# Class tokens of layer 1's feed-forward: both grouped products before their sums over groups, and the output's sums after the first chunk of patches

## The chip, the cores and the metric

The kernel runs on one core of a Trainium2 chip. The core has five engines that work side by side, each through its own queue in order: TensorE (PE; its weight loads are shown apart as PEld), VectorE (DVE), ScalarE (ACT), GpSimd (POOL) and SyncE (SP), which here only issues DMAs. The metric is the device time of one execution in microseconds. The profile is one further execution, recorded by the hardware profiler; times in it count from the start of its span.

## What is computed

The whole program is a network of four layers on a state `x` of 512 nodes by 768 features; each layer has a graph part, an attention part and a feed-forward part. The change lies in the feed-forward part of the second layer, called layer 1. It treats the first six rows (class tokens) and the other 506 rows (patches) differently. Cut to that:

```python
cls_tokens   = x[:, :6]                  # of the normalised x
patch_tokens = x[:, 6:]
patch_out = gelu(patch_tokens @ fc1_w.T + fc1_b) @ fc2_w.T + fc2_b      # 768 -> 192 -> 768
gate_logits = einsum('bnd,nrd->bnr', l2norm(cls_tokens), l2norm(gate_pair)) + balance_bias
route_probs = softmax(gate_logits);  chosen_route = argmax(route_probs)
hid_all = gelu(einsum('bnd,ahd->bnah', cls_tokens, atom_in_w) + atom_in_b)   # five atoms of 192
# the chosen route takes one atom of hid_all, multiplies it by that route's atom_out_w,
# adds atom_out_b, and weighs it with the route's probability
cls_out = chosen_cand * chosen_w
return concatenate([cls_out, patch_out])     # is added to x
```

## The kernel before

**Tiling.** `x` lies token-major: four chunks `t` of 128 tokens, each in two halves `c` of 384 features. Its normalised form `xf` is turned by TensorE into `xfT`, feature-major, six blocks of 128 features (`Norm.first` and `Norm.rest`, two token chunks each; transposes at L274, evacuations at L205 and L207, the scaling itself at L254). All arithmetic is fp32; a matmul shows up as two passes in the trace.

**The class tokens' two products.** Six rows would use only six columns of TensorE. So `in_groups` (L372) deals the terms of a product over three groups of 32 columns: term `k` goes to group `k % 3`, and the three groups accumulate in three strips of one PSUM bank (L377). ScalarE copies the 96 rows to a tile `at_p` (L379). A second, small matmul with the matrix `three` then adds the three strips up (L1680 for the input product, L1771 for the output product), and VectorE adds the result to its place (L1681 to the atoms' `ha`, L1772 to `cls`, which holds the class tokens' rows of `x`). Each product is done in two halves: the input one by 480 of its 960 columns, with six terms each, the output one by 384 of 768 columns, with eleven terms each (ten of 96 rows, from `hT` and the weights `wo`, and one of five rows, the biases, from `cbT`).

**What lies between.** After the input product come the gate (squares L1695, scaling L1701, dot products L1704, softmax and choice to L1716), the coefficients (L1720 to L1723) and the mixing of the atoms (L1749, L1751), nearly all on VectorE with six rows; then ten small transposes (L1757) and a copy (L1758) that make `hT`. The patches' first product, fc1 (L298 and L1738, GELU at L1734 and L1742), gives `hid` beside that.

**The patches' second product.** `from_192` (L314) goes over the four chunks `t`: two matmuls (L320) and two on half of the rows (L323), then `use(t, c, ps)` for both halves: add to `x` (L332), for `t == 0` overwrite the six class rows with `cls` (L1785), and take the statistics of the next norm (L230), after whose second half the norm's small steps follow (L242 to L253) and the scaling on ScalarE (L254). Transposes of the first two chunks (L274) and the products of layer 2's graph part (L557) come next.

**Order, buffers and loads.** Each engine's order is fixed when the program is built, roughly in program order, with ready work drawn forward. PSUM has eight banks, asked for by `psum()`. `at_p` and the rows of biases (`row(...)`, L168) share a pool of two buffers. Weights rotate through three large buffers: the atoms' two input halves, fc1's weights, the atoms' two output halves (L148), fc2's (L1776, L1778), then layer 2's graph weights (L156) and, in one of them, `graph` (L1802). A load waits on SP until the last reader of its buffer is done, and what is behind it on SP waits too. Row `f1_b2` is added to `x` on POOL (L337), chunk by chunk after the chunk's `xf` is made.

Of the kernel before, what the change touches and what calls it, by code (L numbers as in the profile page):

```python
# [22 lines left out]
KC = D // P  # L23
HC = D // 2
# [73 lines left out]
def kernel(ctx: ExitStack, tc: tile.TileContext, a: dict, out: bass.AP):  # L98
    nc = tc.nc
    V, S, G, T = nc.vector, nc.scalar, nc.gpsimd, nc.tensor  # L100
# [20 lines left out]
    def w_tile(name="w", held=None):  # L121
        pool, n = turn_ = turns.pop(0)
        (turns if held is None else held).append(turn_)
        return pool.tile([P, KC * D], FP, tag="w" + n, name=name)

    def psum():
        return psp.tile([P, 512], FP, tag="ps", name="ps")
# [15 lines left out]
    def weights(src, p=P):  # L143

        k, n = src.shape[0] // p, src.shape[1]
        w = w_tile()
        v = w[:, : k * n].rearrange("p (k n) -> p k n", k=k)
        nc.sync.dma_start(v[:p], src.rearrange("(k p) n -> p k n", p=p))  # L148
        return v
# [9 lines left out]
    def spread(src, offset, n, parts=P):  # L159

        return bass.AP(tensor=src.tensor, offset=src.offset + offset, ap=[[0, parts], [1, n]])

    def row_tile(name, n=D):
        return rowp.tile([P, KC * (P + 2)], FP, tag="row", name=name)[:, :n]
# [128 lines left out]
    def feature_product(w, xT, f, width=P):  # L293

        ps = psum()
        n = xT.shape[1]
        for k in range(n):
            T.matmul(ps[:width], w[:, k, f : f + width], xT[:, k, :], start=k == 0, stop=k == n - 1)  # L298
        return ps[:width]

    def token_product(parts, w_of, use, then=None):

        n = len(parts)
        for t in range(NT):
            for c in range(2):
                ps = psum()[:, :HC]
                for k in range(n):
                    T.matmul(ps, parts[k][:, ts(t, P)], w_of(k)[:, ts(c, HC)],  # L308
                             start=k == 0, stop=k == n - 1)
                use(t, c, ps)  # L310
                if then:
                    then(t, c)

    def from_192(hid, wa, wb, use):  # L314


        for t in range(NT):
            bank = [psum()[:, :HC] for _ in range(2)]
            for c in range(2):
                T.matmul(bank[c], hid[:, 0, ts(t, P)], wa[:, ts(c, HC)], start=True, stop=False,  # L320
                         skip_group_check=True)
            for c in range(2):
                T.matmul(bank[c], hid[ts(c, HD), 1, ts(t, P)], wb[ts(c, HD), ts(c, HC)], start=False,  # L323
                         stop=True, skip_group_check=True)
            for c in range(2):
                use(t, c, bank[c])
# [4 lines left out]
    def add_to_x(t, c, ps):  # L331
        V.tensor_add(x[:, t, ts(c, HC)], x[:, t, ts(c, HC)], ps)  # L332
# [28 lines left out]
    G3 = 3 * 32  # L361
    three = const.tile([P, 8], FP, name="three")
# [9 lines left out]
    def in_groups(terms, n, name):  # L372


        ps = psum()[:G3, :n]
        for k, (l, r) in enumerate(terms):
            T.matmul(ps[ts(k % 3, 32)], l, r, start=k < 3, stop=k + 3 >= len(terms), skip_group_check=True)  # L377
        part = row_tile(name, n)
        S.copy(part[:G3], ps)  # L379
        return part[:G3]  # L380
# [804 lines left out]
    xfT, xs, rest = n.T, n.split, n.rest  # L1185
    with tc.tile_pool(name="ffn0", bufs=2) as fp:
# [120 lines left out]
        ps = feature_product(wi, xfT, 2 * P)  # L1307
# [115 lines left out]
    with tc.tile_pool(name="gat1", bufs=1) as gp:  # L1423
# [45 lines left out]
        def use(t, c, ps):  # L1469
            evacuate(h[:, t, 4 * c : 4 * c + 4, :HW], ps.rearrange("p (i c) -> p i c", i=4))  # L1470
# [174 lines left out]
        for t in range(NT):  # L1645
            z = tiny(1, name="ga_z1")
            for c in (1, 0):
                n = HC + c
                ps = psum()[:, :n]
                for s in range(NT):  # L1650
                    T.matmul(ps, ed[0].wT[t][:, s, :], h2[:, s, c * HC : c * HC + n],  # L1651
                             start=s == 0, stop=s == NT - 1)
# [11 lines left out]
    xf, xfT = nf.n, nf.T  # L1664
    with tc.tile_pool(name="ffn1", bufs=1) as fp:
        NCLS, NA, H = 6, 5, 192
        C = NCLS
# [5 lines left out]
        ha = fp.tile([C, NA, H], FP, name="ha")  # L1673
        hf = ha.rearrange("p a h -> p (a h)")
        nc.sync.dma_start(hf, spread(a["L1_ffn_atom_in_b"], 0, NA * H, C))
        for i in range(2):
            w = weights(a["L1_ffn_atom_in_w"][:, ts(i, 480)])
            part = in_groups([(xfT[:, k, :32], w[:, k, :]) for k in range(KC)], 480, "at_p")
            ps = psum()[:C, :480]
            T.matmul(ps, three[:G3, :C], part, start=True, stop=True)  # L1680
            V.tensor_add(hf[:, ts(i, 480)], hf[:, ts(i, 480)], ps)  # L1681
# [51 lines left out]
        ps = feature_product(w1, xfT, 0)  # L1733
        S.activation(hid[:, 0, :], ps, AF.Gelu, bias=col("f1_b1", 0))  # L1734
        ps = psum()[:, :HT]
        for k in range(KC):
            for i in range(2):
                T.matmul(ps[ts(i, HD)], w1[:, k, P : P + HD], xfT[:, k, ts(i, HT)],  # L1738
                         start=k == 0, stop=k == KC - 1, skip_group_check=True)
# [15 lines left out]
        ps = psum()[:HW, : 2 * NA * C].rearrange("p (k n) -> p k n", k=2 * NA)  # L1755
# [3 lines left out]
        cbT = fp.tile([NA, 32], FP, name="cbT")  # L1759
        G.memset(cbT, 0.0)  # L1760
        ps = psum()[:NA, :C]
        T.transpose(ps, cb, ident[:C, :C])
        V.tensor_copy(cbT[:, :C], ps)
        ab = big1[:NA, 0, :]
        nc.sync.dma_start(ab, a["L1_ffn_atom_out_b"])
        wo = [weights(a["L1_ffn_atom_out_w"][i * 480 : (i + 1) * 480, :], HW) for i in range(2)]
        for c in range(2):
            terms = [(hT[:, k, :], wo[k // NA][:HW, k % NA, ts(c, HC)]) for k in range(2 * NA)]
            part = in_groups(terms + [(cbT, ab[:, ts(c, HC)])], HC, "at_p")
            ps = psum()[:C, :HC]  # L1770
            T.matmul(ps, three[:G3, :C], part, start=True, stop=True)  # L1771
            V.tensor_add(cls[:, ts(c, HC)], cls[:, ts(c, HC)], ps)  # L1772


# [7 lines left out]
        def use(t, c, ps):  # L1782
            add_to_x(t, c, ps)
            if t == 0:
                V.tensor_copy(x[:C, 0, ts(c, HC)], cls[:, ts(c, HC)])  # L1785
            n2.part(t, c)

# [83 lines left out]
    xfT, xs, rest = nf.T, nf.split, nf.rest  # L1871
# [106 lines left out]
    xf, xfT = nf.n, nf.T  # L1978
# [7 lines left out]
    with tc.tile_pool(name="ffn3", bufs=1) as fp:  # L1986
# [48 lines left out]
        ps = psum()[:, : NT * E].rearrange("p (t e) -> p t e", t=NT)  # L2035
# [29 lines left out]
        ps = psum()[:, : NT - 1]  # L2065
        for j in range(NT - 1):
            for t in range(NT):
                T.matmul(ps[:, j : j + 1], to_slot[:, t, ts(j, P)], pid[:, t : t + 1],
                         start=t == 0, stop=t == NT - 1, skip_group_check=True)
# [6 lines left out]
        for ks in (range(4), range(4, KC)):  # L2076
            ps = psum()
            for i, k in enumerate(ks):
                for t in range(NT):
                    T.matmul(ps[:, ts(i, P)], xf[:, t, ts(k, P)], to_first[:, t, :],  # L2080
                             start=t == 0, stop=t == NT - 1, skip_group_check=True)
# [174 lines left out]
```

## Time and profile before

| | us |
|---|---|
| median of 3 runs | 3020.36 |
| lowest, highest | 3019.77, 3020.73 |
| the profiled execution | 3019.09 |
| its span | 3017.1 |
| PE busy in the span | 2937.0 |
| L377, the four grouped products: first start to last end | 1668.23 to 1701.63 |
| L320, first start | 1702.99 |
| L557, first product of layer 2's graph part | 1715.80 |

The profiled execution is 1.27 us below the median and 0.7 below the lowest of the timed runs. The stretch that the change touches is some 50 us out of the span. To read the views: the page's first part gives busy time by engine; the chain follows the work that ended last back from release to release, so an engine's share there is time in which the end waited for it; the timeline lists instructions in order of start, with an engine's idle time before one in brackets and what ended it; the windows give busy time by engine in a stretch, and the clock that TensorE was granted (1.00 is full).

### The profile page before, as it was taken

The page shows a single profiled execution, that of the slowest core. Times are in us where ns is not written, and L with a number is a line of the kernel's source. Part 1 is how long each engine was busy: PE and PEld are TensorE (multiplying, and loading weights), DVE is VectorE, ACT ScalarE, POOL GpSimd, SP SyncE. Part 2 cuts the span into 40 slices and gives each one's busy share as a digit, 9 for nine tenths or more (in the row PEclk, how much of TensorE's full clock was granted, in tenths as well). Part 3 has the DMA queues.
Part 4 walks back from the last instruction along what each step waited for, and adds up shares of the span by engine and source line. Part 5 has one row for each costly group of instructions (what it writes and reads, how often), then busy time and mean ns, then how long its engine had stood idle before and what let it go on. Part 6 is the DMA issues. An engine that isn't in the chain of part 4 may idle for free.

```text
span 3017.1 us, 31655 instructions
## 1 busy us (share of the span) xinstructions
PE 2937.0 (97%) x11721; PEld 1979.5 (66%) x11727; DVE 1490.7 (49%) x3446; ACT 754.3 (25%) x1442; POOL 1471.7 (49%) x1568
## 2 busy tenths in 40 slices
PE   7999999999999999999999999999999999999997
PEld 3455555555766776865685457877777776577665
DVE  9845445555356225545677545433333335554234
ACT  7423222241253112103451312200000002122012
POOL 4344444443425565555654543544544557356541
PEclk9999999999999999999999999999999999999999
DMA  3211222221302122322121422221221221232125
GB/s 119 87 48 68 74 74 74 73 95 63 90 16 100 63 94 100 105 96 97 37 90 61 137 99 83 86 89 68 95 94 65 92 94 63 94 121 86 72 94 178
DMA packets 94996, 259.14 MB, mean 86 GB/s; under 512 B 10849, under 2 KB 15841, under 8 KB 93818
## 3 DMA queue, kind: packets, MB, share of 16 engines
q1 hardware_dynamic: 94282, 254.37, 24.1%
q0 software_dynamic: 560, 2.75, 0.3%
q8 instruction: 92, 1.51, 0.2%
q14 instruction: 62, 0.51, 0.1%
HBM read 246.99 MB, written 10.11 MB: 85 GB/s over the span
## 4 chain that ended last, share of the span: by engine, by line
PE 85%; DVE 10%; ACT 2%; POOL 2%; issue 1%; DMA 1%; SPq 0%; POOLq 0%; DVEq 0%; ACTq 0%
PE ps L557 43%; PE ps L652 25%; PE ps L951 5%; DVE oh L752 1%; PE ps L1159 1%; PE ps L1146 1%; PE ps L274 1%; DVE edge_w L801 1%; PE ps L1651 1%; PE ps L308 1%; PE ps L1555 1%; DVE edge_w L803 1%; DVE edge_w L790 1%; PE ps L1392 1%; POOL room L1507 1%
## 5 line engine op out<-in xcount | busy, mean ns | idle before, releaser
L464 POOL TENSOR_TENSOR tw<-w 128x384 f32<-128x384 f32 x246 | 247.6, 1015 | 915.5 <-PE ps L557 245.0
L557 PE MATMUL ps<-sx,w 128*128 128x256 f32 x1188 | 316.5, 380 | 3.0 <-DVE sx L444 2.6
L557 PE MATMUL ps<-sx,tw 128*128 128x256 f32 x1188 | 290.4, 381 | 0.4
L652 PE MATMUL ps<-w,sx 128*128 128x384 f32 x720 | 256.5, 487 | 4.2 <-DVE sx L444 3.0
L468 POOL TENSOR_TENSOR tw<-w 128x384 f32<-128x384 f32 x246 | 252.9, 1034 | 10.3
L470 POOL TENSOR_TENSOR tw<-w,tw 128x384 f32<-128x384 f32 x246 | 251.1, 1027 | 10.4
L466 POOL TENSOR_TENSOR w<-w 128x384 f32<-128x384 f32 x246 | 251.7, 1030 | 9.0
L652 PE MATMUL ps<-tw,sx 128*128 128x384 f32 x720 | 250.5, 488 | 0.2 <-DVE x L701 0.2
L557 PEld LDWEIGHTS ps<-sx,w 128*128 128x128 f32 x1188 | 225.0, 190 | 37.7 <-PE ps L557 2.2
L557 PEld LDWEIGHTS ps<-sx,tw 128*128 128x128 f32 x1188 | 220.0, 190 | 42.7 <-DVE st_u L596 7.2
L572 ACT COPY st_p<-ps 128x256 f32<-128x256 f32 (+1 forms) x127 | 50.0, 394 | 720.0 <-PE ps L557 681.0
L596 DVE TENSOR_TENSOR st_u<-st_p,ps 128x256 f32<-128x256 f32 (+1 forms) x127 | 57.1, 450 | 336.7 <-PE ps L557 336.5
L652 PEld LDWEIGHTS ps<-tw,sx 128*128 128x128 f32 x720 | 136.3, 190 | 95.0 <-DVE x L1928 1.2
L652 PEld LDWEIGHTS ps<-w,sx 128*128 128x128 f32 x720 | 136.7, 190 | 93.9 <-POOL tw L470 4.1
L701 DVE TENSOR_TENSOR x<-x,ps 128x384 f32<-128x384 f32 x216 | 115.2, 552 | 163.4 <-PE ps L652 162.1
L557 PE MATMUL ps<-xfT,w 128*128 128x256 f32 x720 | 176.9, 380 | 0.2
L557 PE MATMUL ps<-w,sx 128*128 128x384 f32 x456 | 167.3, 487 | 2.2 <-DVE ps L600 2.2
L951 PE MATMUL ps<-edge_wT,h 128*128 128x512 f32 x384 | 166.1, 593 | 0.0
L557 PE MATMUL ps<-tw,sx 128*128 128x384 f32 x456 | 162.5, 493 | 3.2 <-DVE st_u L596 3.1
L599 DVE TENSOR_TENSOR st_u<-st_p,ps 128x256 f32<-128x256 f32 (+1 forms) x127 | 57.1, 450 | 205.7 <-PE ps L557 205.7
L557 PEld LDWEIGHTS ps<-xfT,w 128*128 128x128 f32 x720 | 136.3, 190 | 23.8 <-issue 1.3
L652 PE MATMUL ps<-w,hid 128*128 128x384 f32 x432 | 142.9, 488 | 0.0
(535 smaller groups left out, 5034.0 us busy)
## 6 DMA issues: line engine op xcount, KB each, us to landing
w<-in_L_gnn_W SPq DMA_DIRECT2D x60, 768.0 KB, 7.8
w<-in_L_mix_fc_w SPq DMA_DIRECT2D x48, 768.0 KB, 5.9
row<-in_rows SPq DMA_DIRECT2D x39, 384.0 KB, 3.7
w<-in_L_mix_qkv_w SPq DMA_DIRECT2D x18, 768.0 KB, 6.3
w<-in_L_ffn_w SPq DMA_DIRECT2D x18, 768.0 KB, 6.0
w<-in_L_ffn_routed_gate SPq DMA_DIRECT2D x18, 768.0 KB, 6.0
w<-in_L_ffn_routed_up SPq DMA_DIRECT2D x18, 768.0 KB, 6.0
w<-in_L_ffn_routed_down SPq DMA_DIRECT2D x18, 768.0 KB, 7.4
```

Of the source, the lines that this page charges most:

```text
L274: T.transpose(ps[:, j * HT + t * P : j * HT + (t + 1) * P], src[:, 2 * i + t, ts(3 * j + k, P)], ident)
L464: G.tensor_sub(tt[:, 0, k], b22[:, k], b12[:, k])
L466: G.tensor_sub(b12[:, k], b12[:, k], b11[:, k])
L468: G.tensor_sub(tt[:, 1, k], b22[:, k], b12[:, k])
L470: G.tensor_sub(tt[:, 2, k], b21[:, k], tt[:, 1, k])
L557: T.matmul(bank, l, r, start=start and k == 0, stop=stop and k == KC // 2 - 1, skip_group_check=True)
L572: S.copy(b["p1"], b["x"])
L596: V.tensor_add(b["u2"], b["p1r"], b["y"])
L599: V.tensor_add(u3, b["p1r"], b["y"])
L652: T.matmul(b[name], l[:, k, ts(m, P)], r[:, k, :], start=start and k == 0, stop=k == n - 1, skip_group_check=True)
L701: V.tensor_add(x[:, t, ts(j, HC)], x[:, t, ts(j, HC)], ps)
L951: T.matmul(ps, h[:, s, ts(f, P)], wT[:, s, :], start=s == 0, stop=s == NT - 1)
```

## The change

For the input product, both halves' weights are loaded, then both grouped products are issued, then the two sums with their additions to `ha`. For the output product, both grouped products are issued one after the other and their copies kept; sum and addition become a function `class_tokens(c)`, which is called from `use` of chunk 0, after the chunk's own result has been added to `x` and before `cls` is copied over the six rows. No arithmetic is added or taken away.

```diff
-        for i in range(2):
-            w = weights(a["L1_ffn_atom_in_w"][:, ts(i, 480)])
-            part = in_groups([(xfT[:, k, :32], w[:, k, :]) for k in range(KC)], 480, "at_p")
+        at_w = [weights(a["L1_ffn_atom_in_w"][:, ts(i, 480)]) for i in range(2)]
+        parts = [in_groups([(xfT[:, k, :32], w[:, k, :]) for k in range(KC)], 480, "at_p") for w in at_w]
+        for i, part in enumerate(parts):
             ps = psum()[:C, :480]
             T.matmul(ps, three[:G3, :C], part, start=True, stop=True)
             V.tensor_add(hf[:, ts(i, 480)], hf[:, ts(i, 480)], ps)
...
+        parts = []
         for c in range(2):
             terms = [(hT[:, k, :], wo[k // NA][:HW, k % NA, ts(c, HC)]) for k in range(2 * NA)]
-            part = in_groups(terms + [(cbT, ab[:, ts(c, HC)])], HC, "at_p")
+            parts.append(in_groups(terms + [(cbT, ab[:, ts(c, HC)])], HC, "at_p"))
+
+        def class_tokens(c):
             ps = psum()[:C, :HC]
-            T.matmul(ps, three[:G3, :C], part, start=True, stop=True)
+            T.matmul(ps, three[:G3, :C], parts[c], start=True, stop=True)
             V.tensor_add(cls[:, ts(c, HC)], cls[:, ts(c, HC)], ps)
...
         def use(t, c, ps):
             add_to_x(t, c, ps)
             if t == 0:
+                class_tokens(c)
                 V.tensor_copy(x[:C, 0, ts(c, HC)], cls[:, ts(c, HC)])
             n2.part(t, c)
```

## The prediction

> **What bounds the kernel now.** I read the page first: busy time by engine, then the chain that ended last.
>
> ```profile
> PE 2937.0 (97%) x11721; PEld 1979.5 (66%) x11727; DVE 1490.7 (49%) x3446; ACT 754.3 (25%) x1442; POOL 1471.7 (49%) x1568
> ...
> PE 85%; DVE 10%; ACT 2%; POOL 2%; issue 1%; DMA 1%; SPq 0%; POOLq 0%; DVEq 0%; ACTq 0%
> ```
>
> TensorE sets the time; what this change can win is where PE waits in layer 1's feed-forward. So second the chain of waits, in order of time, around it (start, length, what):
>
> ```profile
> 1668.30 2.62 PE ps L377 x12
> ...
> 1670.95 0.56 ACT at_p L379
> ...
> 1671.56 0.97 PE ps L1680 x2
> 1672.53 0.81 PE ps L377 x2
> 1673.33 0.81 PE ps L274 x6
> 1674.14 1.76 PE ps L377 x10
> ...
> 1675.97 0.56 ACT at_p L379
> ...
> 1676.58 0.98 PE ps L1680 x2
> ...
> 1677.59 0.64 DVE ha L1681
> ...
> 1693.81 0.48 ACT at_p L379
> ...
> 1695.78 5.87 PE ps L377 x20
> ...
> 1701.72 0.48 ACT at_p L379
> ...
> 1702.25 0.81 PE ps L1771 x2
> 1703.06 1.49 PE ps L320 x4
> 1704.55 0.90 PE ps L323 x4
> ...
> 1705.50 0.56 DVE x L332
> ```
>
> Four times PE finishes a grouped product (L377), stands still while ScalarE copies it (L379), then sums the groups (L1680, L1771). Nothing else fills these holes; all PE work that asks for a bank later in program order starts after the sum. The timeline gives the holes as 0.64, 0.71, 0.61 and 0.62 us: 2.6 us in all. Between the two pairs (1677.6 to 1688.6) the chain is VectorE's: gate, coefficients, mixed atoms (L1699 to L1758), with fc1's products (L298, L1738, over at 1685.64) beside it. From 1705.5 to 1712.9 it is VectorE again, without a hole: L332, L1785, L230 and the norm's small steps, until the first transposes of the next stage at 1713.98.
>
> Third the windows by stage (length; busy PE, PEld, DVE, ACT, POOL; granted clock; DMA share; GB/s):
>
> ```profile
> 1688.70:1690.00 1.30, 1.27 (x12) 0.63 (x15) 0.00 (x0) 0.00 (x0) 0.00 (x0) 1.00 0.58 158
> 1691.00:1692.00 1.00, 1.00 (x5) 0.01 (x1) 0.00 (x0) 0.00 (x0) 0.00 (x0) 0.50 0.00 0
> 1698.00:1700.00 2.00, 2.00 (x6) 0.52 (x3) 0.00 (x0) 0.00 (x0) 0.00 (x0) 0.50 0.25 37
> 1702.00:1704.00 2.00, 1.75 (x5) 0.77 (x6) 0.54 (x1) 1.48 (x2) 2.00 (x3) 1.00 1.03 407
> ```
>
> Nearly all of both output products runs at half clock: windows of 0.05 us put it from 1690.48 to 1700.72. Three triples of passes before that start 0.32 us apart, those after it 0.64.
>
> **The change, part by part.** Baseline is the profiled execution, 3019.09 us (span 3017.1 and 2.0 around it). It lies 1.27 below the median 3020.36; I subtract the gain from the median.
>
> *A. Input products.* The instructions are the same; the second L377 no longer stands behind the first L1680. Its 12 passes take 4 steps of 0.405 and a tail of 0.57 (the packed ones start at 1674.07, 1674.49, 1674.90, 1675.30), so begun at 1670.9 it is over at 1672.7. If the six late transposes (L274) fall inside it, they wait for the last chunk's xf (ACT L254, ends 1672.43): 1672.45 + 0.88 + about 1.4 = 1674.7. Before it was 1675.87. What is late next is the second copy's place. Both sums' inputs now live at once and the row pool has two buffers; the other holds the row f1_b2, read until here:
>
> ```profile
> 1672.51 2.67 POOL L337 TENSOR_TENSOR x<-x,row 128x384 f32<-128x384 f32 x2 [1.70 <-ACT xf L254]
> ```
>
> That ends at 1675.18. Copy 0.56, gap 0.05, then L1680 from 1675.83 to 1676.80 instead of 1677.55: 0.75 us. If instead the copy takes the first part's buffer, it waits for the first L1680 and can be some 1.5 us sooner still. VectorE idles 1.83 us before the first L1681 at 1672.56 and 0.77 before the second; with both sums later, the squares of L1695 can run there. Should all this idle time be used, the gain is 2.5. Even if the second copy stands ahead of the evacuations L205 on ScalarE, fc1 starts at about 1676.9, not after the old 1677.48. Ends 0 and 2.5; I take **1.1**, near the one waiting place that a row shows. The loads behind it don't move the end: atom_out_w's second half can be issued earlier than 1675.9, but DMA carries some 220 GB/s from 1672 to 1685 either way, and its data is first read after 1689.
>
> *B. First output sum out from between the products.* In the passes one by one, each column group works off its own row: group 0 has terms 0, 3, 6, 9, two passes each, eight steps. L1771's two passes sat in group 0 as well: the second product's group 0 starts at 1695.575, where it could start at 1693.66, when the first product's last pass (1692.89, a step of 0.64) and a weight load (0.13) are through. That is 1.9 us; the last two passes (cbT), which had full clock from 1700.72, would then be at half and give 0.65 back: 1.2 us with the clock unchanged and A at 0. But the clock has its own time. With A the products start at 1687.6; if it still falls at 1690.48, the first product is all but over, the second starts at about 1691.25, eight steps of 0.64 and the tail end at 1698.0. Before: 1701.63. So A and B together 3.7, B **2.6**.
>
> Here a rule bears on it. The Trainium skill, "TensorE: Matmul & The Clock Gate", Part 1, says that the clock is judged in free-running windows of about 3.4 us and that one busy window gives it back. The half-clock stretch is 10.24 us, three such windows; by the records PE was busy 95%, 87% and 100% of them, and only after the third did the clock return. By the rule, without the hole, the first window is full and the clock returns at 1693.90: the second product ends at 1696.0 and B is 4.5. At the row (return no sooner than 1697.31) it is 2.6. I take the row: that first window holds mostly one column group and the five-row cbT passes, so how busy it counts is open. With no fall of the clock at all the products end at 1694.5 and B is 6.0; with it unchanged and A lost, 1.2. Those are the ends.
>
> *C. Second output sum behind the first chunk of patches.* L320 started 1.36 us after the second product's end (copy 0.48, L1771 and gaps); now it follows at once, since hid was ready at 1687.6 and w2's load, issued by 1687.25, finds DMA idle from 1690. **1.36** gained. Cover gone: if w2 or hid were late, PE would wait here, but both have over 5 us to spare.
>
> *D. Sums inside the VectorE stretch.* Two L1772 (542 ns) used to run in VectorE's idle time, at 1695.89 and 1703.10. Now they stand among L332, L1785 and L230, where VectorE is never idle: **-1.08**. L1771 also adds two sums (about 1.3 us at full clock) before the second chunk on PE; VectorE comes to that chunk 1.15 us after PE has it ready (1708.88 against 1707.73) and now 1.1 later, so this is covered. A second rule speaks against this step: the same page ("Architectural detail", in Part 1) has VectorE's queue as a strict FIFO. So L1772 holds up everything behind it until L1771 is through: 1705.23 + 0.33 + 0.48 = 1706.04 on the old scale, and L332 ends at 1706.05. By row and rule together the wait is under **0.1**, as long as PE runs L1771 directly after L323; behind another chunk it is 2.3 a time.
>
> *E. Queues.* Both row buffers are now held until L1771. On SP the loads of g2_b and m2_p (1700.08 and 1703.09) wait for the first and second sum; ahead of them is only the gnn weights' load, released earlier by the second product; behind them Wk, released at 1712.46. The rows are first read at 1718.65. On POOL, graph (L1802, released by L377 at 1700.96) starts earlier with the second product. **0.**
>
> Sum: 1.1 + 2.6 + 1.36 - 1.08 - 0.1 = 3.9 us. 3019.09 - 3.9 = 3015.2 on the profile's scale, **3016.5** on the median's.
>
> **Rivals.**
> - *The clock comes back with the closed hole, or never falls.* For it: the rule, and the busiest window ended the stretch. Against: a stretch at 28.2 to 31.6 ended after a window only 78% busy, so time busy is not the whole measure. At B = 6.0 the gain is 7.3: 3013.1.
> - *The waits are only moved.* VectorE's chain from 1677.6 to 1688.6 is all dependent steps; if the order on its queue puts L1681 no sooner, A is 0, B is 1.2. L1785 took 1.09 us once and 0.33 the other time, beside POOL's tensor operations; twice such a 0.76 more takes 1.5. 1.2 + 1.36 - 1.1 - 1.5 = 0: 3020.4.
> - *Slower: L1771 is queued behind later chunks on PE.* Place: from_192. A chunk is 2.33 us of PE (1702.99 to 1705.32); L1772 waits in VectorE's queue ahead of the norm. Behind all three further chunks the wait is 7.0, net 3.1 lost: 3023.5. It decides from 3.9 us of wait. Against: program order puts the sums ahead of the second chunk, and the transposes and products in the trace keep such order where data are ready.
> - *The order isn't what the text says.* PE already took six transposes out of program order (L274 after the first pass of L377), so the two products may not be adjacent. That is inside A's lower end.
>
> **How the numbers follow.** Forecast (gain 2 to 6, 3014.4 to 3018.4) 0.58; clock rival 0.18; moved waits, and order as before, 0.15; slower 0.09. The range reaches from 3012.5, by the clock rival, to 3021.0, past the moved waits; about 0.15 stays outside. A measurement of this kernel can tell about 0.2% from no change, 6.0 us. Faster by more needs the clock rival and a little of the forecast's upper end: 0.20. Slower by more needs a queue behind later chunks together with a shift elsewhere: 0.08. Within: 0.72.
>
> **What would show it.** Right: L377 x44 without an at_p copy on the chain between; first L1680 after both input products; L320 directly after the last cbT pass; L1771 between L323 and the second L320, L1772 among L332; half-clock stretch shorter or earlier; first L557 of the next stage 3.9 us before 1715.80. Wrong: a wait of L1772 for L1771 over 1 us, a second copy later than 1675.2, L1802 or L156 later than before, or a difference that arises after 1715.8, which nothing here foresees.

## The result and the profile after

| | before | after |
|---|---|---|
| median, us (runs) | 3018.01 (20, with the 3 shown above) | 3025.28 (20) |
| lowest, highest | 3010.85, 3020.92 | 3019.40, 3027.31 |
| profiled execution | 3019.09 | 3025.29 |

The ratio of after to before is 1.0027, with an interval of 1.0021 to 1.0033: 8.1 us slower (6.3 to 10.0); the medians differ by 7.3. Forecast was 3.9 faster. The first views of the page of after, totals and the shares of the chain, hardly move; only ScalarE has an instruction more (1443 against 1442):

```profile
PE 2939.8 (97%) x11721; PEld 1977.7 (65%) x11727; DVE 1490.3 (49%) x3446; ACT 755.8 (25%) x1443; POOL 1471.1 (49%) x1568
...
PE 86%; DVE 9%; ACT 2%; POOL 2%; issue 1%; DMA 1%; SPq 0%; POOLq 0%; DVEq 0%; ACTq 0%
```

Behind the diff, line numbers of after are 3 or 4 higher (L1771 is now L1774). Its chain of waits through the stage (start, length, what):

```profile
1671.12 0.56 ACT at_p L379
...
1671.73 0.97 PE ps L1680 x2
1672.70 5.35 PE ps L298 x12
1678.04 2.77 PE ps L1738 x24
...
1682.30 0.47 ACT hid L1742
...
1682.79 1.28 ACT L1710
...
1684.08 0.21 ACT lo L1710
...
1689.68 0.32 PE ps L1757 x2
...
1690.35 13.38 PE ps L377 x44
1703.74 2.86 PE ps L320 x4
1706.60 1.02 PE ps L323 x4
1707.62 1.39 PE ps L1774 x4
```

On TensorE the edit did nearly what it says: the second input product no longer waits for the first sum (the first L1680, at 1669.92, runs beside that product's last passes, the second follows at 1671.73 after its copy), the output products are one block of 44 passes that waits for no copy, the patches' product (L320) follows at once, and the first output sums come directly behind chunk 0. But the chain now goes through fc1, its GELUs (L1742) and a nameless 1.28 us of ScalarE before the gate's Exp (L1710). Fc1 used to run beside the gate; now the gate waits for it.

ScalarE's timeline shows why (start, length, line, operation, idle time before and what ended it). Before:

```profile
1676.43 0.20 ACT L1697 ACTIVATE ss<-ss 6x3 f32<-6x3 f32 x1
1676.64 1.28 ACT L1725 ACT_TABLE_LOAD   x1
1678.26 1.00 ACT L1725 ACTIVATE ha<-ha 6x960 f32<-6x960 f32 x1 [0.34 <-DVE ha L1681]
1679.28 1.28 ACT L1710 ACT_TABLE_LOAD   x1
1682.53 0.20 ACT L1710 ACTIVATE lo<-lo 6x2 f32<-6x2 f32 x1 [1.96 <-DVE lo L1709]
1682.74 1.28 ACT L1734 ACT_TABLE_LOAD   x1
1684.04 0.69 ACT L1734 ACTIVATE hid<-ps,cols 128x512 f32<-128x512 f32 x1
```

After:

```profile
1671.69 1.28 ACT L1725 ACT_TABLE_LOAD   x1
1673.41 1.00 ACT L1725 ACTIVATE ha<-ha 6x960 f32<-6x960 f32 x1 [0.44 <-DVE ha L1681]
1674.43 1.28 ACT L1697 ACT_TABLE_LOAD   x1
1675.73 0.20 ACT L1697 ACTIVATE ss<-ss 6x3 f32<-6x3 f32 x1
1675.95 1.28 ACT L1734 ACT_TABLE_LOAD   x1
1678.08 0.69 ACT L1734 ACTIVATE hid<-ps,cols 128x512 f32<-128x512 f32 x1 [0.85 <-PE ps L298]
1680.83 1.94 ACT L1742 ACTIVATE hid<-ps,b 64x256 f32<-64x256 f32 x4 [2.06 <-PE ps L1738]
1682.79 1.28 ACT L1710 ACT_TABLE_LOAD   x1
1684.08 0.20 ACT L1710 ACTIVATE lo<-lo 6x2 f32<-6x2 f32 x1
```

Before, the order was the gate's Sqrt (L1697), the atoms' GELU (L1725), the gate's Exp, fc1's GELUs. After, it is the atoms' GELU, Sqrt, fc1's GELUs, Exp. In these rows each change among Sqrt, GELU and Exp comes with a table load of 1.28 us, and the new order has one more (four against three). VectorE's timelines hold the cause and the price. Before:

```profile
1675.24 0.93 DVE L1695 SCALAR_TENSOR_TENSOR cls<-cls 6x768 f32<-6x768 f32 x1
...
1677.59 0.64 DVE L1681 TENSOR_TENSOR ha<-ha,ps 6x480 f32<-6x480 f32 x1 [0.77 <-PE ps L1680]
```

After:

```profile
1668.27 0.94 DVE L1695 SCALAR_TENSOR_TENSOR cls<-cls 6x768 f32<-6x768 f32 x1 [0.92 <-DMA cls<-in_L_ffn_gate_pair]
...
1672.73 0.64 DVE L1681 TENSOR_TENSOR ha<-ha,ps 6x480 f32<-6x480 f32 x1 [1.10 <-PE ps L1680]
1673.31 0.94 DVE L1695 SCALAR_TENSOR_TENSOR cls<-cls 6x768 f32<-6x768 f32 x1
...
1684.32 0.14 DVE L1711 TENSOR_REDUCE mx<-lo 6x1 f32<-6x2 f32 x1 [3.82 <-ACT lo L1710]
```

The second addition to `ha` (L1681) now stands ahead of the gate's third square (L1695, at 1673.31); before, it stood behind it (at 1675.24). So what the atoms' GELU needs is ready before what the Sqrt needs, and the order that is built swaps them; the Exp falls behind all of fc1. (That readiness decides the swap, and the Exp's place too, is read from the orders and not shown; the sums behind the square without the order held weren't tried.) VectorE waits 3.82 us for it.

The other loss is the clock. Windows of TensorE in after, set on the boundaries at which the clock changes (stretch; length, busy PE; granted clock; DMA share; GB/s):

```profile
1679.63:1683.04 3.41, 1.16 (x12) 1.00 0.95 223
1683.04:1686.45 3.41, 0.00 (x0) 0.50 0.46 148
1686.45:1689.87 3.42, 1.41 (x11) 0.50 0.02 5
1689.87:1693.28 3.41, 3.05 (x17) 0.50 0.00 0
1693.28:1696.69 3.41, 3.41 (x10) 0.50 0.00 0
1696.69:1700.11 3.42, 3.42 (x16) 0.50 0.00 0
1700.11:1703.52 3.41, 3.41 (x10) 0.50 0.75 233
1703.52:1706.93 3.41, 3.41 (x7) 0.50 1.03 407
1706.94:1710.35 3.41, 3.41 (x12) 1.00 0.39 120
```

Half clock lasts seven windows of 3.41 us, where before had three. It starts while PE waits for the gate, and both output products and the first patches product run in it.

**Measuring a stage.** Executions of one kernel differ by some 10 us, and the time goes with the clock: of the 53 runs of before taken beside the second set of experiments, the 17 with a mean granted clock of 0.993 have a mean span of 3017.5 us, the 10 with 0.996 one of 3011.1. So one profile's total says little about an edit worth 4 us. Below, places in the stage are counted from the first of its transposes (L274, at 1666.18 before and 1662.79 after), up to the next stage's first product (L557): 49.62 us before, 55.66 after. The two spans (3017.1 and 3023.5) differ by 6.4; ahead of the stage and behind it they differ by 3.4 and 3.7 in opposite directions, in instructions that stand in the same order. There the clock explains it: ahead, before has five windows of half clock and after three, behind it two and four (and both one at the very end), and two windows at half speed are 3.4 us. Where the rest of the 8.1 lies, one profile can't say. The median of before beside the three sets of experiments was 3018.75, 3017.97 and 3017.57 us.

### The profile page after: what moved, and what is told of

It is laid out like the page before. It is cut to its first block, busy times and chain, and to the rows that moved or that the text cites. A ratio compares the mean times of both kernels' runs of the same rounds, so it can differ in the third digit from the quotient of the medians.

```text
span 3023.5 us, 31658 instructions
## 1 busy us (share of the span) xinstructions
PE 2939.8 (97%) x11721; PEld 1977.7 (65%) x11727; DVE 1490.3 (49%) x3446; ACT 755.8 (25%) x1443; POOL 1471.1 (49%) x1568
## 4 chain that ended last, share of the span: by engine, by line
PE 86%; DVE 9%; ACT 2%; POOL 2%; issue 1%; DMA 1%; SPq 0%; POOLq 0%; DVEq 0%; ACTq 0%
PE ps L557 43%; PE ps L652 25%; PE ps L951 5%; PE ps L1159 1%; DVE oh L752 1%; PE ps L1146 1%; PE ps L274 1%; DVE edge_w L801 1%; PE ps L298 1%; PE ps L1651 1%; PE ps L308 1%; PE ps L1555 1%; DVE edge_w L803 1%; DVE edge_w L790 1%; PE ps L1392 1%
## 5 line engine op out<-in xcount | busy, mean ns | idle before, releaser
L557 PE MATMUL ps<-sx,w 128*128 128x256 f32 x1188 | 316.2, 380 | 3.0 <-DVE sx L444 2.6
L557 PE MATMUL ps<-sx,tw 128*128 128x256 f32 x1188 | 290.5, 381 | 0.6
L557 PEld LDWEIGHTS ps<-sx,w 128*128 128x128 f32 x1188 | 224.5, 190 | 38.2 <-PE ps L557 2.2
L557 PEld LDWEIGHTS ps<-sx,tw 128*128 128x128 f32 x1188 | 219.4, 190 | 44.0 <-DVE st_u L596 8.2
L557 PE MATMUL ps<-xfT,w 128*128 128x256 f32 x720 | 176.9, 380 | 0.2
L557 PE MATMUL ps<-w,sx 128*128 128x384 f32 x456 | 167.2, 487 | 2.2 <-DVE ps L600 2.2
L557 PE MATMUL ps<-tw,sx 128*128 128x384 f32 x456 | 161.9, 491 | 3.2 <-DVE st_u L596 3.1
L557 PEld LDWEIGHTS ps<-xfT,w 128*128 128x128 f32 x720 | 135.8, 190 | 24.4 <-issue 1.3
```

The source lines that it names most:

```text
L557: T.matmul(bank, l, r, start=start and k == 0, stop=stop and k == KC // 2 - 1, skip_group_check=True)
```

## The experiments

The theory: grouping the input products turns ScalarE's order round, and the clock enlarges the loss. Rivals: the output part costs the time (its sums in VectorE's stretch, or behind other work on PE); or the order matters little and the clock is all.

**Each part alone.** `e1_in` takes the first hunk of the diff, `e2_out` the other two.

> Only the input product's part of the change; the output part as before. Theory 1 (Exp of the gate, L1710, falls behind fc1's GELUs on ScalarE's queue once the input products stand together): slower than before by 5 to 9 us, Exp again after 1683 in the profile, PE idle for some 6 us before the small transposes L1757. Theory 2 (the output's sums inside VectorE's norm stretch make the loss): within 1.5 us of before.

> Only the output product's part of the change; the input part as before. Theory 1: not slower; faster by 1 to 4 us, since the two holes behind the output products are gone (1.2 to 2.6 and 1.4) and two sums of 0.54 are added to VectorE's stretch. Theory 2: slower by 5 us or more.

Measured: `e1_in` 3024.45 us, ratio 1.0017 (1.0007 to 1.0026). ScalarE has after's new order, the output products begin at 27.53 as in after (27.56; before 22.55). `e2_out` 3020.96, ratio 1.0006 (0.9999 to 1.0013): ScalarE as before, products from 22.57, and L320 follows 0.07 before their last pass ends. The loss comes with the input part, some 5 us of it (2.1 to 7.8). But the output part alone missed the gain of 1 to 4 that was expected: its half clock lasted five windows where before had three.

**ScalarE's order.** `e3_after_exp` is the change with fc1's GELUs held behind the Exp; `e4_before_flip` is before with nothing but the Exp, and the VectorE steps that follow it (L1711 to L1723), moved behind fc1's last GELU; `e5_after_both` is the change with both places as before.

```diff
+        def behind(first):        # holds the latest instruction behind another of its engine
+            tc.add_manual_dep(nc.cur_bb.bb.instructions[-1], first.name, mybir.DependencyInfo(
+                mybir.DependencyClass.NoSync, mybir.DependencyReason.DATA), reason="pinned")
...
+        gate_sqrt = nc.cur_bb.bb.instructions[-1]      # after the Sqrt; e5 only
...
+        gate_exp = nc.cur_bb.bb.instructions[-1]       # after the Exp; e3 and e5
...
+        behind(gate_sqrt)                              # the atoms' GELU; e5 only
...
+        behind(gate_exp)                               # each of fc1's GELUs; e3 and e5
...
+        last_gelu = nc.cur_bb.bb.instructions[-1]      # after fc1's last GELU; e4 only
+        S.activation(lo, lo, AF.Exp)
+        behind(last_gelu)
```

> The whole change, with one order set by hand: fc1's GELUs (L1734, L1742) behind the gate's Exp on ScalarE. Theory 1: the loss is gone; faster than before by 1 to 5 us, the wait of VectorE for Exp under 1 us instead of 3.8. Theory 2: as the changed kernel, slower by about 7 us.

> The kernel before, with nothing of the change, but the gate's Exp behind fc1's last GELU on ScalarE. Theory 1: slower by 4 to 8 us: hid's last GELU ends at 1687.6 in the trace of before, a table load of 1.28 and Exp follow, so L1711 starts at about 1689.1 instead of 1682.8 (6.3 us), and the half-clock stretch can grow. Theory 2: within 1.5 us of before.

> The whole change, with ScalarE's order from the square root to fc1's last GELU set as it was before (Sqrt, GELU of the atoms, Exp, GELUs of hid). If the rest of the loss in the last run but one (first transpose of xf to first output product 24.1 us against 22.6) is the square root behind the atoms' GELU and its table load, that stretch falls to 21.5 to 22.6 us, and the time to within 3 us of before. If it is something else in the input part, it stays near 24.

Measured: `e3_after_exp` 3022.17, 1.0015 (1.0008 to 1.0021), Exp at 17.85, products from 24.12. The start is 3.44 us better than in after, but the gain that was expected did not come: the Sqrt still stands behind the atoms' GELU, and half clock lasts six windows. `e4_before_flip` 3022.70, 1.0021 (1.0012 to 1.0029), Exp at 22.74, products from 29.01: the late Exp alone, with none of the change's edits, costs 6.3 us (3.6 to 8.8; in its profile the stage is 4.15 longer, 53.77). `e5_after_both` 3013.51, 0.9989 (0.9982 to 0.9996): 3.3 us faster than before (1.2 to 5.4), products from 22.57. Its ScalarE timeline (line numbers 4 to 7 higher than in before):

```profile
1673.35 0.20 ACT L1701 ACTIVATE ss<-ss 6x3 f32<-6x3 f32 x1 [2.61 <-DVE cls L1699]
...
1674.87 1.00 ACT L1731 ACTIVATE ha<-ha 6x960 f32<-6x960 f32 x1
...
1678.15 0.20 ACT L1715 ACTIVATE lo<-lo 6x2 f32<-6x2 f32 x1 [0.98 <-DVE lo L1714]
...
1679.67 0.69 ACT L1741 ACTIVATE hid<-ps,cols 128x512 f32<-128x512 f32 x1
```

Sqrt, atoms' GELU, Exp, fc1's GELU again. Same arithmetic, same order on TensorE as in after; the sign of the change turns with two places in another engine's queue. The Exp's place is worth 27.56 - 24.12 = 3.44 us of start, the Sqrt's 24.12 - 22.57 = 1.55.

**The clock.** Products of 384 columns from `xfT` into a bank that nobody reads are laid before and between the ten small transposes (L1757), so that PE has no long holes there: twelve in `e6_after_warm`, six in `e7_both_warm` (on top of e5), `e8_before_warm` (on top of before) and `e9_out_warm` (on top of e2).

```diff
+        filler = psum()
+        def fill(first):
+            T.matmul(filler[:, :HC], ident, xfT[:, 0, :HC], start=True, stop=True)
+            if first:
+                behind(first)
+        for _ in range(2):                             # 8 in e6
+            fill(None)
...
+            if k % 2 and k < 2 * NA - 1:               # behind every second transpose
+                fill(nc.cur_bb.bb.instructions[-1])
```

> The whole change, and TensorE given products of no use (identity times xfT, 384 columns) while it waits for VectorE between fc1 and the output products: eight before the small transposes, one between each pair. ScalarE's order stays as in the changed kernel. If half of the products' 13.4 us is the clock that fell in the 6 us of idle time: both output products in 7 to 9 us instead of 13.4, first chunk of patches at full clock, 5 to 7 us faster than the changed kernel, so about as before. If the clock is not what makes them long: no gain, or a loss by what the fillers delay.

> The whole change, ScalarE's order as before, and the fillers (two before the small transposes, one between each pair). If order and clock are the whole of the loss: faster than before by 4 to 8 us. If the sums in VectorE's stretch cost more than their 1.1 us: less than 3 us faster.

> The kernel before with the fillers alone. If the half-clock stretch of 10 us there costs what the passes' starts say (0.64 instead of 0.32 us a step, some 14 steps): faster than before by 3 to 5 us. The difference to the run before it is then what the change is worth at full clock: 1 to 3 us.

> The output part of the change alone (the input products as before), with six products of 384 columns that compute nothing used, laid on TensorE before and between the output products so that its clock does not fall. Theory (order on ScalarE as before; what the output part alone did not bring was lost to the clock): no half clock, output products in about 7.0 us, the patches' product directly behind them, next stage's first product about 13.3 after it; from the first transpose of xf to the next stage's first product about 45.8, against 48.05 of the kernel before with the same six products: 2.2 us faster than that one, some 2 faster than the kernel before. Rival (the output part is worth nothing even at full clock, because its sums in VectorE's stretch give it back): 48.0, and the time of the kernel before with the fillers.

Measured: no half clock in the stage in any of the four profiles. (The profile of e5 is of its fastest execution, that of e6 of its slowest; so stages are compared here, not spans.)

| kernel | output products from | their length | then to L320 | L320 to L557 | all | us | ratio to before |
|---|---|---|---|---|---|---|---|
| before | 22.55 | 12.90 | 1.36 | 12.81 | 49.62 | | |
| after | 27.56 | 13.38 | -0.07 | 14.79 | 55.66 | 3025.28 | 1.0027 |
| e8, before at full clock | 25.61 | 8.28 | 1.36 | 12.80 | 48.05 | 3018.18 | 0.9996 (0.9987 to 1.0004) |
| e9, output part | 25.63 | 6.98 | -0.07 | 13.28 | 45.82 | 3016.37 | 0.9997 (0.9989 to 1.0006) |
| e6, after | 28.88 | 6.98 | -0.07 | 13.28 | 49.07 | 3018.93 | 1.0004 (0.9995 to 1.0012) |
| e7, order as before | 24.32 | 6.98 | -0.07 | 13.28 | 44.51 | 3012.72 | 0.9986 (0.9978 to 0.9993) |

The fillers themselves take 1.3 to 3.1 us of the start. From the start of the products to L557 before needs 22.44 us at full clock and the change 20.19: the output part is worth 2.25. After's order costs 49.07 - 44.51 = 4.56 us with the clock out of the way (e6, e7). The end times of e8 and e9 don't resolve these 2 us: their ratios are the same within the intervals. Expected were gains of 3 to 5 for e8 and some 2 for e9; the fillers of each take 3.06 of it away. Against the full-clock lengths, after's stage loses 55.66 - 27.56 - 20.19 = 7.91 us to the clock, before's 49.62 - 22.55 - 22.44 = 4.63. So the 6.04 us come apart: start 5.01, output part -2.25, clock 3.28; each of these rests on one profile of each kernel.

**The third square.** In e5 the products begin no sooner than before (22.57 against 22.55), though the input products end 1.58 us sooner. `e10_squares` is e5 with the two input sums (L1680, L1681) moved in the text behind the squares, ahead of the Sqrt, so that VectorE doesn't wait for a sum before the third square. `e11_squares_warm` adds six fillers of 320 columns. `e12_squares_again` is e10 once more, on another chip, for a second profile.

```diff
-        for i, part in enumerate(parts):
-            ps = psum()[:C, :480]
-            T.matmul(ps, three[:G3, :C], part, start=True, stop=True)
-            V.tensor_add(hf[:, ts(i, 480)], hf[:, ts(i, 480)], ps)
...
+        for i, part in enumerate(parts):
...
         S.activation(ss, ss, AF.Sqrt)
```

> The change with ScalarE's order held as before (Sqrt, GELU ha, Exp, fc1's GELUs), and the two sums of the input product moved in the text behind the squares of the gate, so that VectorE does the third square before it waits for the first sum. Theory (the input part gains nothing on the chain because the third square stands behind both additions to ha): the Sqrt starts 1 to 1.5 us sooner after the first transpose of xf than with the order held alone (10.0 to 10.5 instead of 11.49), Exp at 15.0 to 15.5 instead of 16.29, output products from 21.3 to 21.7 instead of 22.57; the time about 1 us below that of the change with the order held (some 0.9985 of before). Rival (the gate's dot products wait for something else): output products from 22.5 as before, same time as with the order held.

> The same as the run with the squares ahead of the input sums, and six products of 320 columns, not used, that keep TensorE's clock up before and between the output products. Theory (waits and clock add up): no half clock, products in 6.9 us or less, next stage's first product 43 to 43.6 after the first transpose of xf, against 44.51 without the moved squares and 49.62 before: 0.9978 to 0.9984 of the kernel before, the fastest of all. Rival (the gain is taken up by the fillers or by what comes after): 44.5, 0.9986.

> The kernel with the squares ahead of the input sums once more, for a second profile: the first was of its fastest execution (3008.13 us, granted clock 0.997), while its median is 3020.95 at a mean clock of 0.993. Theory (the waits are gone in every execution, and the clock takes the gain back in most): Sqrt, Exp and the output products begin at the same places after the first transpose of xf as in the first profile (9.2, 15.1, 21.3, within 0.3), but half clock covers the products or the first chunk, so that the next stage's first product comes 45 to 51 after it instead of 41.46, with a time of 3016 to 3024. Rival (the time is lost in another stage): next stage's first product at 41.5 again, and a longer rest of the span.

Measured: in e10 the Sqrt is at 9.17, the Exp at 15.07, the products begin at 21.29: 1.28 us sooner than in e5, and in its profile no half clock falls in the stage: L557 at 41.46. That is 8.16 us less than before: 1.26 of start, 2.25 of the output part, and the 4.63 that before loses to the clock. Yet its median is 3020.95 and its ratio 1.0013 (1.0004 to 1.0021): slower than before. The profiled execution was its fastest, 3008.13 us. The second profile (3020.54 us) has Sqrt at 9.16, Exp at 15.06, products from 21.27, all within 0.02, and L557 at 49.41. Windows of TensorE in that second profile:

```profile
1682.13:1685.54 3.41, 1.73 (x17) 1.00 0.96 262
1685.54:1688.95 3.41, 3.06 (x17) 0.50 0.31 81
1688.95:1692.37 3.42, 3.42 (x10) 0.50 0.00 0
1692.37:1695.78 3.41, 3.41 (x16) 0.50 0.00 0
1695.78:1699.19 3.41, 3.41 (x10) 0.50 0.76 241
1699.19:1702.61 3.42, 3.42 (x7) 0.50 1.03 411
1702.61:1706.02 3.41, 3.41 (x12) 1.00 0.38 120
```

And in the first:

```profile
1679.43:1682.84 3.41, 2.24 (x22) 1.00 0.95 212
1682.84:1686.26 3.42, 2.55 (x23) 1.00 0.61 183
1686.26:1689.67 3.41, 3.41 (x25) 1.00 0.00 0
```

Same kernel, same holes. Against the stage the boundaries lie 0.89 us apart. In one execution they cut the transposes' stretch so that no window is less than 66% busy, and the clock stays; in the other a window holds 1.73 us of work, 51%, and five windows of half clock follow; the stages differ by 7.95 us. The mean clocks of e10's 19 timed runs suggest that the second is the rule: 15 at 0.991 to 0.993, 4 at 0.994 to 0.997. With the fillers (`e11_squares_warm`) the stage is 43.72 and the time 3012.40 us, 0.9984 (0.9976 to 0.9993), over 3010.45 to 3014.99, where e10 spreads over 3008.13 to 3024.33. It is the fastest version by median and faster than before and after; the intervals of e5, e7 and e11 overlap.

## Why the prediction was wrong

It named the right holes; what it didn't look at was whether another engine's order stays. Its baseline was off besides: the median of three runs, 3020.36, lies 2.35 above that of twenty.

**A, input products: the step that failed.** "The instructions are the same; the second L377 no longer stands behind the first L1680" was followed through TensorE, the copies and VectorE, and the steps up to there hold: the second copy ends its wait for POOL's L337, as the prediction put it, and the second addition to `ha` comes at 9.94 instead of 11.41, 1.47 us sooner (0.75 was worked out; L337 itself took 1.97 instead of 2.67). Then "with both sums later, the squares of L1695 can run there" is half right: the second square moved there (1668.27), but the third got behind both additions, and with it the Sqrt. No step asked which of ScalarE's two waiting functions would now be ready first. What it put at nothing, without a reason, is the place of the Exp on ScalarE: VectorE waits 3.82 us for it in after, 0.27 in before. Worth of A: forecast 1.1 sooner, measured 5.01 later (e5 and e3: 3.44 for the Exp, 1.55 for the Sqrt). With the order held it is 0 (e5: 22.57), the lower end and the value of the rival of moved waits. With the squares taken out of the way too (e10) it is 1.26, close to the 1.1, but that takes edits which the change doesn't have. The rival "the order isn't what the text says" pointed at TensorE's order and was bounded at 0: the mechanism was thought of and put on the wrong engine.

**B, first output sum: right mechanism, wrong about the clock.** At full clock the two products are 8.28 - 6.98 = 1.30 us shorter (e8 and e9), near the 1.2 given as "the clock unchanged"; but that was worked out at half clock, so the agreement proves little. The 2.6 taken came from letting the products run ahead of the fall of the clock. They ran into it: the wait for the Exp makes a hole of 6.2 us on PE, the clock falls before they begin, and they take 13.38 us instead of 12.90. In e5, without that hole, the clock fell too, 2.0 us before the products (1682.42 against 1684.42), but came back after two windows, and they took 9.34. The rule of the Trainium skill, "TensorE: Matmul & The Clock Gate", Part 1, as it was weighed there, that one busy window of 3.4 us gives the clock back, is not enough by the records: in after four windows in a row are 100% busy before the clock returns behind the fourth. In before, e4 and e5 the first 100% window ended the half clock, as by the rule. The row, return no sooner than 1697.31, was one execution's, and no sounder an end.

**C, second output sum: right.** 1.36 forecast; 1.36 + 0.07 = 1.43 measured in after, e2, e5, e6, e7 and e9.

**D, sums in VectorE's stretch: right mechanism, too large.** 1.08 and 0.1 forecast; at full clock L320 to L557 grew from 12.80 to 13.28, 0.48. Each added sum lengthens the chain by 0.46 to 0.47 us in e5, its 0.54 less the overlap with its neighbours; and the first copy of `cls` over `x` takes 0.65 us there where it took 1.09 before. What shortened the copy wasn't tried. The wait for the sum that could have been 2.3 did not come: L1774 runs directly behind L323.

**E, queues: 0, as forecast**; with the order held, nothing in the stage is late.

B, C and D together came to 2.78 in the forecast and 2.25 at full clock. That the forecast 3.9 as a whole is near what e5 gave (3.3, 1.2 to 5.4) is luck in part, for the shares are others: A at 0 and a shorter half clock. Of the rivals none had the mechanism; the slower one (3023.5, by L1771 behind later chunks on PE) came near the time, but looked at the wrong queue.

## What to carry to other kernels

Before an edit that moves when results are ready, list for every engine whose order is built from readiness the instructions that stand close together, above all functions of ScalarE that need different tables: here two functions changed places when their inputs became ready in another order, and an Exp of 0.2 us came 5 us later. Compare the engines' orders of before and after first, all of them, and only then the times; where one turned, hold it by a dependency and measure again. And where a stage has TensorE waiting for some 1 to 6 us, a gain in waits can be lost to the clock: look at half-clock windows in several executions, and try filling the holes (e11 gained by it against e10; e8 did not against before, for its fillers delayed the products).

## What the hardware showed that was not expected

**The clock's windows.** Half-clock stretches in these profiles are whole multiples of 3.41 us (but for the last, which the end of the execution cuts), on boundaries that stay fixed within an execution and differ between executions; with the stage's work alike, e10's stage took 41.46 us in one execution and 49.41 in another. PE's busy share of a window by the records doesn't decide fall or return alone: windows 34% (after), 51% (e12) and 66% (before, ahead of 1690.48) busy were followed by a fall, windows of 66% and 75% (e10) were not; the first 100% busy window brought the clock back in before, e4 and e5, the second in e1, only the fourth in after, e3 and e12, and the fifth in e2. What is counted stays open.

**A change of table** costs 1.31 us here from the last GELU's end to the Exp's start (1682.77 to 1684.08). The Trainium skill, "ScalarE: Activation LUTs", "What ACT_TABLE_LOAD costs", gives 1.28 for the load, which agrees, and a drain of 1.38 on top, which no row of these profiles shows.
